# Block maxima in a table in one PSUM bank, with seven banks left for everything else

## Chip, cores and metric

The kernel runs on one core of one Trainium2 chip. The metric is the device time of one execution in microseconds (us); three runs of the kernel before took 3574.15, 3577.49 and 3579.05 us, so the median is 3577.49. The engines are TensorE (PE: matmuls; PEld: its weight loads), VectorE (DVE), ScalarE (ACT), GpSimd (POOL) and SyncE (SP, which issues most DMAs). TensorE writes its results to PSUM, which has eight banks of 512 fp32 columns by 128 partitions; VectorE and ScalarE read and write PSUM, GpSimd does not in this kernel.

## Reference

Four cross-attention layers in a row on a state `x` of 4 batches x 512 positions x 256 channels, all in fp32, all against one context of 1024 positions x 512 channels for each batch. Layers 0, 2 and 3 are alike: 16 heads of 64, with a bias on a few context positions.

```python
q = hidden_states @ Wq                       # 256 -> 16 * 64
k = encoder_hidden_states @ Wk               # 512 -> 16 * 64
v = encoder_hidden_states @ Wv
logits = jnp.einsum('bhqd,bhkd->bhqk', q, k) * scale
logits = logits + col_bias[None, None, :, :]
probs = jax.nn.softmax(logits, axis=-1)
out = jnp.einsum('bhqk,bhkd->bhqd', probs, v)
...
out = out @ Wo + bo + residual
```

Layer 1 normalises `x` by its root mean square first and has 16 query heads of 16 in 4 groups, each group with one key and value head ("grouped" attention). It has no bias on positions.

The softmax needs a number to subtract before the exponential. Any number that is the same for all 1024 context positions of one query and head will do, if it keeps the exponentials in range. This kernel takes a maximum.

## The kernel before

**Units.** A unit is two heads of a masked layer (0, 2, 3), or four heads of the grouped layer done as two runs of the same shape; a layer of a batch has eight units, so there are 96 masked and 32 grouped units (`units`, L44). A unit's logits are kept transposed: context positions on the partitions, in eight blocks of 128 (`NT`), and in a block 1024 columns, 512 queries for each of two heads. So one block of one unit is a tile of 128x1024, two PSUM banks.

**Steps.** The kernel is one long list of 96 steps, written out by hand (`order`, L70, and the loop at L1183). In step n the masked unit `g` is scored, the masked unit of the step before, `g1`, is attended, and weights and projections for later units fill TensorE's time. In 32 of the steps (12 to 19, 22 to 29, 32 to 39, 68 to 75) a grouped unit `lam` is attended too, and in most of these the logits of the next grouped unit, `coming`, are made. Each engine runs its instructions in the order in which the program issues them. The loop holds an estimated clock `now`: the items of `fill` run one after the other, subtractions and exponentials are issued as `events` when `now` passes their due time, logits pairs (`pairs`) are due from 12.0 on, 2.5 apart, and the work in `late` (scaling of attention outputs) is issued when the events are through, at the first logits pair or at the end of the step.

**One masked unit, in the order of a step:**
- `scores` (L832): for each of the eight blocks a matmul for each head into a pair of banks (L841), for block 0 also the bias (L847), a copy to SBUF by ScalarE (`g.st[t]`, L851). Block 0's pair is kept: VectorE takes the maximum of it and each later block in place (L855).
- `max_quarters` (L896) makes one maximum out of that pair for each 32 columns: L892 reduces 1024 columns to 32 with a 32x32 transposition, and seven small instructions (L902 to L909) combine the four quarters of the partitions. `max_everywhere` (L912) spreads the result over a pair of banks (L918), the "broadcast".
- `subtract` (L922): VectorE subtracts the broadcast from each block (L926); after the eighth the pair is given back. `exponentials` (L930): ScalarE (L932), and GpSimd adds the blocks up (L971).
- In the next step `attend` (L861): 16 matmuls into one bank, `g.po` (L871). Then, as `late` work, `normalise` (L1017): the sums are reduced in the same way as the maxima (`reciprocal_sums`, L892 and L1003 to L1011), spread (L1013), and the output is scaled (L1024), which gives `g.po` back.
- Two steps later `project_out` (L1027): two units together into a pair of banks (L1042), and VectorE adds the result to the state (L1060 or L1064).

**One grouped unit**: `logits_pair` (L813) makes two blocks at once, with two pairs of banks (L818), copies them (L824) and takes the maximum in place (L830); GpSimd subtracts (L924); `attend` puts it into one bank; `keep_even` (L881) and `keep_odd` (L883, L885) add the two halves of the output, and after every second unit `turn_grouped` (L973) divides by the sums, by transposing the output into a bank of its own and back (L982 to L988), and issues one or four DMAs on SP.

**Fill.** Projections of queries (`project_q`, L736), of keys (`k_part`, L525: four matmuls into one bank, in two items) and of values (`v_pair`, L571: likewise one bank for two items). In steps 41 to 64 and 77 to 92 keys and values of two units are made by seven products in place of eight from combined weights and contexts (`seven_products`, L624, L639); these hold two or three single banks at once.

**Banks.** All of PSUM is one tensor, `ps_all`. A `Place` (L101) takes one bank or an aligned pair, `back` gives it back. Both happen while the program is written, so the choice is fixed; on the chip the first writer of a bank waits until the last reader of its former use is done. The chooser takes what was given back longest ago:

```python
if width == 2:
    at = min(
        (n for n in range(0, 8, 2) if n in free and n + 1 in free),
        key=lambda n: max(free[n], free[n + 1]),
    )
else:
    at = min(free, key=lambda n: free[n] + (2 if n ^ 1 in free else 0))
```

`free` maps a bank to the count of returns at which it came back; a single bank whose neighbour is free too is put two returns later. Ties go to the bank that came back first.

Of the kernel before, what the change touches and what calls it, by code (L numbers as in the profile page):

```python
# [12 lines left out]
ALU = mybir.AluOpType  # L13
AX = mybir.AxisListType
PSUM = bass.MemoryType.PSUM

P = 128
B, S, C = 4, 512, 256
T, CT = 1024, 512
NI = S // P  # L20
NT = T // P
# [59 lines left out]
def kernel(ctx: ExitStack, tc: tile.TileContext, a: dict, out: bass.AP):  # L81
    nc = tc.nc
# [8 lines left out]
    def t_(shape, tag, name, bufs=1, dtype=FP):  # L91
        return sb.tile(shape, dtype, tag=tag, name=name, bufs=bufs)
# [2 lines left out]


    ps_all = ps.tile([P, 8, S], FP, tag="ps", name="ps")
    given_back = dict.fromkeys(range(8), 0)
    returns = [0]

    class Place:  # L101
# [26 lines left out]
    def take_set(g):  # L128
        g.set = sets_free.pop(sets_free.index(min(sets_free)))
        g.st = [st_slot((NT + 1) * g.set + t) for t in range(NT)]  # L130
        g.mx = st_slot((NT + 1) * g.set + NT)
# [681 lines left out]
    def logits_pair(g, i):  # L813
        ws = [Place(), Place()]
        for odd in range(2):
            for j in range(2):
                rows = slice(64 * odd + 32 * j, 64 * odd + 32 * (j + 1))
                nc.tensor.matmul(  # L818
                    ws[odd].ap[:, j * S : (j + 1) * S], lhsT=g.kt[rows, i * P : (i + 1) * P],
                    rhs=g.qt[rows, :], start=True, stop=True,  # L820
                )
        for odd, w in enumerate(ws):
            t = 2 * i + odd
            nc.scalar.copy(g.st[t], w.ap)  # L824
            if t == 0:
                g.mx_place = w
            else:
                w.back()
                top = g.mx_place.ap
                nc.vector.tensor_tensor(top, top, g.st[t], ALU.max)  # L830

    def scores(g):  # L832
        take_set(g)
        g.mx_place = Place()
        for t in range(NT):

            w = Place() if t else g.mx_place
            m = w.ap
            keys = slice(t * P, (t + 1) * P)
            for j in range(2):  # L840
                nc.tensor.matmul(  # L841
                    m[:, j * S : (j + 1) * S], lhsT=g.kt[g.rows[j], keys], rhs=g.qt[g.rows[j], :],
                    start=True, stop=t > 0,
                )
            if t == 0:
                for j in range(2):
                    nc.tensor.matmul(  # L847
                        m[:, j * S : (j + 1) * S], lhsT=aug_k[g.l][g.rows[j], keys],
                        rhs=aug_q[g.rows[j], :], start=False, stop=True,
                    )  # L850
            nc.scalar.copy(g.st[t], m)  # L851
            if t:
                w.back()
                top = g.mx_place.ap
                nc.vector.tensor_tensor(top, top, g.st[t], ALU.max)  # L855

    def place_out(g, width=1):
        g.place = Place(width)
# [24 lines left out]
    def keep_odd(g):  # L883
        half = gq[g.b, "o"][64 * g.h : 64 * (g.h + 1), :]
        nc.vector.tensor_tensor(half, half, g.po[64:128, :], ALU.add)  # L885
        g.place.back()

    def over_quarter(out_, of, op):
        nc.vector.tensor_reduce(  # L892
            out_, of.rearrange("p (b x) -> p b x", x=32), AX.X, op, apply_transpose=True
        )

    def max_quarters(g):  # L896
        w = Place(1)
        quarter, half = w.ap[:, 0:32], w.ap[0:64, 32:64]
        other = t_([64, 32], "other_max", f"other_max_{g.name}")
        over_quarter(quarter, g.mx_place.ap, ALU.max)  # L900
        g.mx_place.back()
        nc.vector.tensor_copy(other, quarter[64:128, :])  # L902
        nc.vector.tensor_tensor(half, quarter[0:64, :], other, ALU.max)
        nc.vector.tensor_copy(other[0:32, :], half[32:64, :])
        g.every = t_([P, 2 * S // 32, 1], "every", f"every_{g.name}")
        for h in range(4):
            nc.vector.tensor_tensor(  # L907
                g.every[32 * h : 32 * (h + 1), :, 0], half[0:32, :], other[0:32, :], ALU.max
            )  # L909
        w.back()  # L910

    def max_everywhere(g):  # L912
        if g.masked:
# [57 lines left out]
        nc.gpsimd.tensor_tensor(g.acc, g.st[0] if t == 1 else g.acc, g.st[t], ALU.add)  # L971

    def turn_grouped(g):  # L973
        w = Place(1)
        normalise_grouped(g, w.ap)
        w.back()

    def normalise_grouped(g, m):

        o = gq[g.b, "o"]  # L980
        short = t_([P, S // 32, 1], "short", f"short_{g.name}")
        nc.vector.transpose(m, o)  # L982
        nc.vector.reciprocal(short, m.rearrange("p (c r) -> p c r", r=32)[:, :, 16:17])
        nc.vector.transpose(
            m.rearrange("p (c r) -> p c r", r=32), short.to_broadcast([P, S // 32, 32])
        )
        g.ot = o
        nc.vector.tensor_tensor(o, o, m, ALU.mult)  # L988
        if g.u % 4 == 1:
            nc.sync.dma_start(out=o_kept, in_=o)  # L990
        else:
            for i in range(4):
                nc.sync.dma_start(
                    out=o[32 * i + 16 : 32 * (i + 1), :], in_=o_kept[32 * i : 32 * i + 16, :]
                )

    def reciprocal_sums(g, m):

        quarter, half = m[:, 0:32], m[0:64, 32:64]
        other = t_([64, 32], "other", f"other_{g.name}")  # L1000
        short = t_([P, S // 32, 1], "short", f"short_{g.name}")
        over_quarter(quarter, g.acc, ALU.add)
        nc.vector.tensor_copy(other, quarter[64:128, :])  # L1003
        nc.vector.tensor_tensor(half, quarter[0:64, :], other, ALU.add)
        nc.vector.tensor_copy(other[0:32, :], half[32:64, :])
        for h in range(4):
            cols = slice(h // 2 * S // 32, (h // 2 + 1) * S // 32)
            nc.vector.tensor_tensor(
                short[32 * h : 32 * (h + 1), :, 0], half[0:32, cols], other[0:32, cols], ALU.add
            )  # L1010
        nc.vector.reciprocal(short, short)  # L1011
        g.ot = t_([P, S], "ot", f"ot_{g.name}", bufs=3)
        nc.vector.transpose(  # L1013
            g.ot.rearrange("p (c r) -> p c r", r=32), short.to_broadcast([P, S // 32, 32])
        )

    def normalise(g):  # L1017
        w = Place(1)
        reciprocal_sums(g, w.ap)
        w.back()  # L1020
        scale_out(g)

    def scale_out(g):
        nc.vector.tensor_tensor(g.ot, g.po, g.ot, ALU.mult)  # L1024
        g.place.back()
# [76 lines left out]
    def at(n):  # L1102
        return steps[n] if 0 <= n < len(steps) else (None, None)
# [79 lines left out]
    for n in range(len(steps) + 2):  # L1183
        g, lam = at(n)
# [74 lines left out]
        def pair(i):  # L1259
            if i == 0:  # L1260
                behind_exponentials()
                take_set(coming)
            logits_pair(coming, i)
            if i == NT // 2 - 1:
                max_quarters(coming)
                max_everywhere(coming)
# [11 lines left out]
        if g:  # L1278
            g.now = NT if masked_at(g.n + 1) else 4
            scores(g)  # L1280
# [5 lines left out]
        if g:  # L1286
            max_quarters(g)
            max_everywhere(g)
        if g1 and g:
            attend(g1)  # L1290
            give_set(g1)
            if not ending:
                late.append(lambda: normalise(g1))
        elif g1:
            attend_last(g1)
            adds = [project_out(*each) for each in outs]
            outs = []
            reciprocal_rows(g1.ot, g1.psum, g1.mx)
            scale_out(g1)
            for add in adds:  # L1300
                add()
# [42 lines left out]
        if lam:  # L1344

            def attend_grouped():
                while any(of is lam for _, of, _ in events):
                    events.pop(0)[2]()
                lam.v = head(lam).v
                place_out(lam)  # L1350
                attend(lam)
                give_set(lam)
                late.append(lambda: keep_odd(lam))
                if lam.h == 1:
                    late.append(lambda: turn_grouped(lam))
# [81 lines left out]
```

## Time and profile before

| | us |
|---|---|
| median of three runs | 3577.49 |
| the profiled execution, as timed | 3576.7 |
| its span in the profile | 3574.9 |
| TensorE busy | 3470.4 |
| VectorE busy | 3036.3 |
| GpSimd busy | 2488.9 |
| ScalarE busy | 2331.6 |

The profiled execution lies within the runs. Lengths of steps, from one bias matmul (L847) to the next: 28.7 us for the plain even steps 42 to 64, 31.7 to 33.7 for the odd ones between, 40 to 42 for even steps with a grouped unit, 50 to 53 for odd ones.

The blocks of instructions of the change, from the groups by line (count, mean ns):

| line | what | count | mean |
|---|---|---|---|
| L855, L830 | maximum of two blocks, in place in PSUM | 672 + 224 | 1232, 1233 |
| L892 | reduction of 1024 columns from PSUM (maxima) | 128 | 1265 |
| L892 | the same from SBUF (sums) | 93 | 1253 |
| L902 to L904 | quarters of the maxima | 3 x 128 | 181 to 193 |
| L907 | last step of the quarters | 512 | 180 |
| L982, L984 | turning the grouped output | 16 each | 727 |

In the views below a line of a group reads: line, engine, operation, what it writes from what, shapes, count, busy us, mean ns, idle time of the engine ahead of it and who ended that. A line of the timeline reads: start us, length us, engine, line, operation, count of merged instructions, and in brackets the idle time ahead of the first. A line of the waits reads: who waited, for whom, us in total, times, longest.

### The profile page before, as it was taken

The page shows a single profiled execution, that of the slowest core. Times are in us where ns is not written, and L with a number is a line of the kernel's source. Part 1 is how long each engine was busy: PE and PEld are TensorE (multiplying, and loading weights), DVE is VectorE, ACT ScalarE, POOL GpSimd, SP SyncE. Part 2 cuts the span into 40 slices and gives each one's busy share as a digit, 9 for nine tenths or more (in the row PEclk, how much of TensorE's full clock was granted, in tenths as well). Part 3 has the DMA queues.
Part 4 walks back from the last instruction along what each step waited for, and adds up shares of the span by engine and source line. Part 5 has one row for each costly group of instructions (what it writes and reads, how often), then busy time and mean ns, then how long its engine had stood idle before and what let it go on. Part 6 is the DMA issues. An engine that isn't in the chain of part 4 may idle for free.

```text
span 3574.9 us, 42639 instructions
## 1 busy us (share of the span) xinstructions
PE 3470.4 (97%) x15262; PEld 1701.6 (48%) x15262; DVE 3036.3 (85%) x4166; ACT 2331.6 (65%) x2701; POOL 2488.9 (70%) x1241
## 2 busy tenths in 40 slices
PE   8999999999999999999999999999999999999998
PEld 4454544445444454444454545454544445454553
DVE  7778788887888878898888888888789888888887
ACT  4565577775777757777566666665677775666664
POOL 3565477774777747777678778767477776769774
PEclk9999999999999999999999999999999999999999
DMA  3222201002100030101001111010201011002110
GB/s 102 62 87 89 75 18 51 27 20 72 42 27 27 20 93 21 27 27 44 29 27 51 33 33 51 27 48 24 69 25 45 26 36 46 23 27 74 33 31 7
DMA packets 146201, 151.70 MB, mean 42 GB/s; under 512 B 23608, under 2 KB 123448, under 8 KB 145476
## 3 DMA queue, kind: packets, MB, share of 16 engines
q1 hardware_dynamic: 142894, 140.05, 12.6%
q0 software_dynamic: 2560, 8.39, 0.7%
q8 instruction: 121, 1.98, 0.2%
q14 instruction: 92, 0.75, 0.1%
q10 hardware_dynamic: 534, 0.52, 0.1%
HBM read 132.15 MB, written 15.73 MB: 41 GB/s over the span
## 4 chain that ended last, share of the span: by engine, by line
PE 78%; DVE 18%; ACT 2%; issue 2%; POOL 0%; DMA 0%; DVEq 0%; ACTq 0%; POOLq 0%
PE ps L871 16%; PE ps L841 15%; PE ps L639 13%; PE ps L584 10%; PE ps L536 10%; PE ps L818 5%; DVE st L926 5%; DVE ps L855 5%; PE ps L742 4%; PE ps L1042 3%; DVE ps L892 2%; DVE ps L830 1%; DVE every L907 1%; PE ps L719 1%; DVE ps L918 1%
## 5 line engine op out<-in xcount | busy, mean ns | idle before, releaser
L971 POOL TENSOR_TENSOR st<-st 128x1024 f32<-128x1024 f32 x668 | 1580.6, 2366 | 687.9 <-ACT st L932 643.0
L932 ACT ACTIVATE st<-st 128x1024 f32<-128x1024 f32 x1024 | 1037.0, 1056 | 320.7 <-DVE st L926 238.9
L855 DVE TENSOR_TENSOR ps<-ps,st 128x1024 f32<-128x1024 f32 x672 | 827.6, 1232 | 258.3 <-ACT st L851 197.4
L926 DVE TENSOR_TENSOR st<-st,ps 128x1024 f32<-128x1024 f32 x768 | 883.4, 1215 | 3.3
L924 POOL TENSOR_TENSOR st<-st 128x1024 f32<-128x1024 f32 x256 | 597.3, 2381 | 354.4 <-DVE st L918 306.1
L871 PE MATMUL ps<-st,v 128*64 128x512 f32 (+1 forms) x4064 | 790.9, 596 | 0.0
L851 ACT COPY st<-ps 128x1024 f32<-128x1024 f32 x768 | 717.1, 1046 | 104.3 <-PE ps L847 62.7
L841 PE MATMUL ps<-qt,kt 64*128 64x512 f32 x3072 | 723.5, 604 | 42.6 <-DVE ps L892 25.5
L841 PEld LDWEIGHTS ps<-qt,kt 64*128 64x128 f32 x3072 | 307.1, 187 | 401.2 <-issue 123.2
L871 PEld LDWEIGHTS ps<-st,v 128*64 128x64 f32 (+1 forms) x4064 | 240.8, 130 | 528.4 <-issue 428.3
L536 PE MATMUL ps<-ctx,wk 128*128 128x512 f32 x896 | 425.8, 624 | 2.2 <-ACT ctx L416 2.2
L584 PE MATMUL ps<-wv,ctx 128*128 128x256 f32 x1792 | 405.9, 382 | 0.0
L830 DVE TENSOR_TENSOR ps<-ps,st 128x1024 f32<-128x1024 f32 x224 | 276.1, 1233 | 144.3 <-ACT st L824 134.1
L584 PEld LDWEIGHTS ps<-wv,ctx 128*128 128x128 f32 x1792 | 336.8, 190 | 96.1 <-issue 53.3
L824 ACT COPY st<-ps 128x1024 f32<-128x1024 f32 x256 | 247.6, 1014 | 130.7 <-PE ps L818 129.0
L536 PEld LDWEIGHTS ps<-ctx,wk 128*128 128x128 f32 x896 | 171.9, 198 | 247.3 <-issue 231.0
L639 PE MATMUL ps<-st 128*128 128x128 f32 (+1 forms) x1200 | 229.0, 339 | 6.3 <-ACT ps L662 6.3
L818 PE MATMUL ps<-qt,kt 32*128 32x512 f32 x1024 | 196.4, 666 | 29.7 <-DVE ot L1024 24.9
L654 ACT COPY st<-ps 128x512 f32<-128x512 f32 x40 | 23.4, 585 | 301.6 <-PE ps L639 301.6
L639 PEld LDWEIGHTS ps<-st 128*128 128x128 f32 x1200 | 158.7, 192 | 74.7 <-issue 68.7
L742 PE MATMUL ps<-x,wq 128*128 128x512 f32 x384 | 186.6, 609 | 4.0 <-ACT st L824 2.3
L1042 PE MATMUL ps<-ot,wo 128*128 128x512 f32 x384 | 175.8, 600 | 0.7 <-DVE ot L1024 0.7
(178 smaller groups left out, 2740.5 us busy)
## 6 DMA issues: line engine op xcount, KB each, us to landing
ctx<-kept SPq DMA_DIRECT2D x24, 1024.0 KB
wk<-in_L_xattn_Wk_dram SPq DMA_DIRECT2D x47, 512.0 KB
wv<-in_L_xattn_Wv_dram SPq DMA_DIRECT2D x47, 512.0 KB
wq<-in_L_xattn_Wq_dram SPq DMA_DIRECT2D x96, 128.0 KB
wo<-in_L_xattn_Wo_dram SPq DMA_DIRECT2D x96, 128.0 KB
st<-kept SPq DMA_DIRECT2D x4, 2048.0 KB
qt<-q SPq DMA_DIRECT2D x64, 128.0 KB
kept<-st SPq DMA_DIRECT2D x12, 512.0 KB
```

The lines of the kernel that those rows point to most:

```text
L536: nc.tensor.matmul(m, lhsT=g.w["k"][:, k, :], rhs=ctx_half[g.b, n][:, k, :], start=(k == 0), stop=(k == KT - 1),)
L584: nc.tensor.matmul(m[:, half * 2 * P : (half + 1) * 2 * P], lhsT=ctx_half[g.b, t // 4][:, k, t % 4 * P : (t % 4 + 1) * P], rhs=g.w["v2"][: ...
L639: nc.tensor.matmul(m if is_keys else m[:, q], lhsT=right[:, k, :] if is_keys else left_[:, k, q], rhs=left_[:, k, :] if is_keys else right ...
L818: nc.tensor.matmul(ws[odd].ap[:, j * S : (j + 1) * S], lhsT=g.kt[rows, i * P : (i + 1) * P], rhs=g.qt[rows, :], start=True, stop=True,)
L841: nc.tensor.matmul(m[:, j * S : (j + 1) * S], lhsT=g.kt[g.rows[j], keys], rhs=g.qt[g.rows[j], :], start=True, stop=t > 0,)
L851: nc.scalar.copy(g.st[t], m)
L855: nc.vector.tensor_tensor(top, top, g.st[t], ALU.max)
L871: nc.tensor.matmul(g.po[at, :], lhsT=g.v[:, t, rows], rhs=g.st[t][:, j * S : (j + 1) * S], start=(t == first), stop=(t == last),)
L924: nc.gpsimd.tensor_tensor(g.st[t], g.st[t], g.mb, ALU.subtract)
L926: nc.vector.tensor_tensor(g.st[t], g.st[t], g.mb, ALU.subtract)
L932: nc.scalar.activation(st, st, AF.Exp)
L971: nc.gpsimd.tensor_tensor(g.acc, g.st[0] if t == 1 else g.acc, g.st[t], ALU.add)
```

## The change

One PSUM bank, number 7, is taken out of the chooser. Its first 256 columns are a table `tops` of 32 x 8, and four areas of 32 columns follow for the small trees. Each block's maxima are reduced at once, from the copy in SBUF, into column t of the table (`block_max`); the pair of banks of block 0 is given back like all others. `max_quarters` reduces the table (256 columns to 32) and takes no bank, `reciprocal_sums` takes none either. `turn_grouped` uses the bank of the grouped unit's own output, which `keep_odd` therefore gives back only for the first unit of two.

```diff
-    given_back = dict.fromkeys(range(8), 0)
+    given_back = dict.fromkeys(range(7), 0)
...
@@ logits_pair
             nc.scalar.copy(g.st[t], w.ap)
-            if t == 0:
-                g.mx_place = w
-            else:
-                w.back()
-                top = g.mx_place.ap
-                nc.vector.tensor_tensor(top, top, g.st[t], ALU.max)
+            w.back()
+            block_max(g, t)
...
     def scores(g):
         take_set(g)
-        g.mx_place = Place()
         for t in range(NT):
-
-            w = Place() if t else g.mx_place
+            w = Place()
...
             nc.scalar.copy(g.st[t], m)
-            if t:
-                w.back()
-                top = g.mx_place.ap
-                nc.vector.tensor_tensor(top, top, g.st[t], ALU.max)
+            w.back()
+            block_max(g, t)
...
     def keep_odd(g):
         half = gq[g.b, "o"][64 * g.h : 64 * (g.h + 1), :]
         nc.vector.tensor_tensor(half, half, g.po[64:128, :], ALU.add)
-        g.place.back()
+        if g.h == 0:
+            g.place.back()
...
+    tops = ps_all[:, 7, 0:256].rearrange("p (b t) -> p b t", t=NT)
+    most, most_half, added, added_half = (
+        ps_all[:, 7, 256 + 32 * n : 288 + 32 * n] for n in range(4)
+    )
...
+    def block_max(g, t):
+        over_quarter(tops[:, :, t], g.st[t], ALU.max)
+
     def max_quarters(g):
-        w = Place(1)
-        quarter, half = w.ap[:, 0:32], w.ap[0:64, 32:64]
+        g.every = t_([P, 2 * S // 32, 1], "every", f"every_{g.name}")
+        quarter, half = most, most_half[0:64, :]
         other = t_([64, 32], "other_max", f"other_max_{g.name}")
-        over_quarter(quarter, g.mx_place.ap, ALU.max)
-        g.mx_place.back()
+        nc.vector.tensor_reduce(quarter, tops, AX.X, ALU.max)
...
-        w.back()
...
     def turn_grouped(g):
-        w = Place(1)
-        normalise_grouped(g, w.ap)
-        w.back()
+        normalise_grouped(g, g.place.ap)
+        g.place.back()
...
-    def reciprocal_sums(g, m):
-        quarter, half = m[:, 0:32], m[0:64, 32:64]
+    def reciprocal_sums(g):
+        quarter, half = added, added_half[0:64, :]
...
     def normalise(g):
-        w = Place(1)
-        reciprocal_sums(g, w.ap)
-        w.back()
+        reciprocal_sums(g)
         scale_out(g)
```

`over_quarter` (L891) is unchanged: `nc.vector.tensor_reduce` of 1024 columns in groups of 32 with a transposition. `normalise_grouped` (L978) is unchanged too.

More of the change, by code (lines that the diff above doesn't have):

```diff
@@ L904, in max_quarters @@
         nc.vector.tensor_copy(other[0:32, :], half[32:64, :])
-        g.every = t_([P, 2 * S // 32, 1], "every", f"every_{g.name}")
         for h in range(4):
```

## The prediction

> **What bounds the kernel now.** I read the page's totals and chain first, then TensorE's waits, then step by step the granted clock, and last the timeline around the longest waits.
>
> ```profile
> span 3574.9 us, 42639 instructions
> PE 3470.4 (97%) x15262; PEld 1701.6 (48%) x15262; DVE 3036.3 (85%) x4166; ACT 2331.6 (65%) x2701; POOL 2488.9 (70%) x1241
> ...
> PE 78%; DVE 18%; ACT 2%; issue 2%; POOL 0%; DMA 0%; DVEq 0%; ACTq 0%; POOLq 0%
> ```
>
> TensorE sets the end, and VectorE is the one engine that interrupts it. TensorE's idle time is 104.5 us (3574.9 less 3470.4). Most of it has four causes, in the waits of TensorE (total, times, longest):
>
> ```profile
> PE ps L841 <- DVE ps L892: 25.5, 17, 1.8
> PE ps L818 <- DVE ot L1024: 24.9, 12, 2.8
> PE ps L841 <- ACT st L824: 11.4, 12, 1.0
> PE ps L818 <- DVE o L885: 4.8, 4, 1.4
> ```
>
> All four are waits for a PSUM bank. The first: the scores of a masked unit (L841) need the pair of banks in which the running maximum of the grouped unit still stands, until L892 has read it. The second: the logits of a grouped unit (L818) need the bank of the attention output, until L1024 has scaled it. I asked for the twelve odd steps in which a grouped unit is attended and another one's logits are made (13, 15, 17; 23, 25, 27; 33, 35, 37; 69, 71, 73), each from one bias matmul L847 to the next:
>
> ```profile
> 1476.90:1528.90 52.00, 47.12 (x178) 17.04 (x176) 44.63 (x61) 34.30 (x38) 35.16 (x15) 0.93 0.07 16
> ...
> sum 620.30, PE 572.27 PEld 209.31 DVE 534.59 ACT 413.40 POOL 421.99; mean PE 47.69 PEld 17.44 DVE 44.55 ACT 34.45 POOL 35.17
> ```
>
> The columns are length, busy time of the five engines, granted clock, DMA. TensorE is idle for 48.0 us in these twelve steps, and its clock is 0.93 in ten of them and 0.97 in two, where other steps have 1.00: 10 x 52 x 0.07 + 2 x 50 x 0.03 = 39 us lost. The timeline of one such step (start, length) shows both:
>
> ```profile
> 1475.90 1.13 PE L841 MATMUL ps<-qt,kt 64*128 64x512 f32 x4 [0.95 <-ACT st L824]
> ...
> 1479.87 1.13 PE L841 MATMUL ps<-qt,kt 64*128 64x512 f32 x4 [1.77 <-DVE ps L892]
> ...
> 1482.56 9.22 DVE L855 TENSOR_TENSOR ps<-ps,st 128x1024 f32<-128x1024 f32 x7
> ...
> 1510.86 2.79 PE L818 MATMUL ps<-qt,kt 32*128 32x512 f32 x4 [2.77 <-DVE ot L1024]
> ...
> 1513.58 3.47 PE L536 MATMUL ps<-ctx,wk 128*128 128x512 f32 x4
> ```
>
> After the wait of 2.77 us four matmuls take 3.47 us, which take 1.98 us elsewhere: the clock has dropped. The masked steps without a grouped unit (41 to 64, 77 to 92) have hardly any idle time and can't gain.
>
> **VectorE's tree, old and new.** Per group of eight blocks the old tree is seven L855 (or L830) and one L892; the new one is eight reductions of 128x1024 from SBUF and one of 256 elements.
>
> ```profile
> L926 DVE TENSOR_TENSOR st<-st,ps 128x1024 f32<-128x1024 f32 x768 | 883.4, 1215 | 3.3
> L855 DVE TENSOR_TENSOR ps<-ps,st 128x1024 f32<-128x1024 f32 x672 | 827.6, 1232 | 258.3 <-ACT st L851 197.4 <-DVE ps L855 0.9 <-ACT st L932 0.5
> ...
> L892 DVE TRANSPOSE_TENSOR_REDUCE ps<-ps 128x32 f32<-128x1024 f32 x128 | 161.9, 1265 | 12.1
> L892 DVE TRANSPOSE_TENSOR_REDUCE ps<-st 128x32 f32<-128x1024 f32 x93 | 116.5, 1253 | 3.9 <-ACT kt L541 3.9
> ...
> L226 DVE TENSOR_REDUCE first<-st 128x12 f32<-128x144 f32 x1 | 0.3, 303 | 0.0
> ```
>
> The block reduction costs 1253 ns (the sum's L892 reads SBUF likewise). The last reduction isn't in the trace: no less than L226's 303 ns (144 elements), no more than 1253 (1024). L226 is nearest; with the slope from L251 (12 elements, 165 ns) to it, 1.05 ns an element, 256 make 420 ns, an estimate. In durations: 8 x 1.253 + 0.42 = 10.44 us against 7 x 1.232 + 1.265 = 9.89, so 0.55 us more a group, 70 us over 128 groups, on an engine 85% busy.
>
> The distance between instructions decides more. Seven L855 back to back take 9.22 us: each starts (9.22 - 1.232) / 6 = 1.331 us after the last, 0.10 more than its duration, because it reads what that one wrote. Eight L926, independent, take 9.14 us in the step after: 1.132 apart, 0.08 less than their duration. A block reduction writes a column of its own and reads nothing of its predecessor. If it runs like L926 it comes every 1.17 us, if like L855 every 1.36. I take 1.17, since the dependency that stretches L855 is gone, and keep 1.36 for the range. Then a backlogged tree lasts 8 x 1.17 + 0.08 + 0.03 + 0.42 = 9.9 us instead of 10.6 (L855's start to L892's end): 0.7 earlier, and the grouped unit's tail ahead of it (1.25 + 0.42 behind the last copy, instead of 1.23 + 1.27) another 0.8. With 1.36 the tree is 0.7 us longer and the two cancel.
>
> The Trainium skill speaks against this edit (VectorE: DVE Perf Modes, "The DRAIN you can't avoid"): VectorE flushes its pipeline after each instruction whether a semaphore follows or not, so one should count instructions. Nine in place of eight would then lose 0.55 us a group; by that rule L885 would come no earlier, the even steps below would pay 34 us instead of 14 and the products 18 instead of none, and the sum would be 3560. The rows of L926 disagree: they overlap by 83 ns.
>
> **Banks.** I followed the chooser (lines 102-119) by hand with seven banks. The scores use three pairs in turn, as before, but no pair is held by a maximum. The attention output takes bank 6, the only one without a free neighbour. The broadcast maximum takes the pair of block 5, so until the last subtraction L926 the fill has two pairs where it had two pairs and a single.
> - Start of odd steps: the pair under L892 doesn't exist any more, and the first scores find the third pair free. The waits for L892 (25.5) and for L824 (11.4) go. L892's cover in the old code was none: TensorE stood.
> - Logits in odd steps: the first call gets the keys' pair, long copied out, and the broadcast's. The wait for L1024 goes, but the pair is free only after the last subtraction (0.3 us of waiting), and the second call takes the same two pairs again and waits for ScalarE's copies, which stand behind the exponentials: by the timeline some 1.5 us. 12 x 1.8 = 22 us come back. In steps 23 and 71, where the projection of queries goes to the end of the fill, that call meets the grouped output's bank, given back only after the turning (L988, 2.6 us behind L885): 2 x 4 = 8.
> - Logits in even steps: by a tie the grouped output lands in the queries' pair, and the second block waits for keep_odd (L885), which it didn't before:
>
> ```profile
> 1463.50 1.94 PE L818 MATMUL ps<-qt,kt 32*128 32x512 f32 x8
> ...
> 1466.12 0.69 DVE L885 TENSOR_TENSOR o<-o,ps 64x512 f32<-64x512 f32 x1
> ```
>
> L885 ends at 1466.81, and 1.6 us earlier with the shorter tree: 1465.2. The first block is through at 1464.0. 12 steps x 1.2 = 14 us. Behind the waiting L818 on TensorE stand the value products L584 and the other logits, and ScalarE's L824 and the block reductions wait for it in turn; with some 2 us of slack before the next step's tree they come late by no more than the wait itself.
> - Products with combined weights in the thirteen odd steps that don't load a new context: the second product now falls into the bank of the output projection and waits for its addition on VectorE:
>
> ```profile
> 1818.68 1.88 PE L639 MATMUL ps<-ctx,wk 128*128 128x512 f32 x4
> ...
> 1819.32 1.40 DVE L1060 SCALAR_TENSOR_TENSOR x<-ps,colL_xattn_bo,x 128x512 f32<-128x512 f32 x2
> ```
>
> The product starts at 1818.68. The first addition ends 0.70 us after 1819.32, 1.3 too late; in steps with L1064 it is 1.9. In these steps the tree starts with block 0's copy, 1 us earlier than now, and ends 1.7 us earlier: nothing to some 0.2 us remains. Without that gain (1.36) it costs 18 us.
> - The quarters' and the turning's own banks fall away: TensorE's waits for L907 (4.0 us) go. The turning keeps the grouped bank 2.6 us longer, counted above. No DMA moves, and SP's queue has the same issues behind L988.
>
> **Sum.** Against: 48.0 idle and 39 of clock in the odd steps, 11.4 at their starts (ahead of L847, so not in the 48), 7 for the four L892 waits in steps 19, 29, 39 and 75, 4.8 for L885: 110 us. Left or new: 22 + 8 + 14 = 44, and the clock. Waits of 1.4 us in the even steps drop no clock now, waits of 0.93 in the odd ones mostly do, so half of those steps pay 2 to 3 us again: 15. Gain 110 - 59 = 51, with 4 for L907: 55 us. The profiled execution took 3576.7 us (span 3574.9 and 1.8 around it), 0.8 below the median of 3577.49: **3522 us**. Its own range is 3485 (the new waits don't show) to 3555.
>
> **Rivals.**
> - VectorE waits for itself between block reductions, as at L855 (1.36 apart). For it: all eight write one bank, and the program may order accesses by bank; VectorE is 86% busy in the odd steps (534.59 of 620.30). Against: no read follows. The wait sits in every tree and decides from 1.3 us apart. L885 is then 1.6 us later: 12 x 2.8 = 34 in the even steps, the odd ones wait for the last subtraction 12 x 1.6 more = 19, 18 at the products, all the clock loss stays (39, and 15 more in the even steps), besides 44 - 14 = 30. 114 - 155 = -41: 3618, slower.
> - The waits move more than I count: the tree is quick, but ScalarE's copies, L885 and L988 hold TensorE half as long again (66 us for 44), and the clock pays 20 for 15. 114 - 86 = 28: 3549. For it: VectorE and ScalarE are both full around the first logits. Against: the copies alone need 1.93 us a pair, which the fill between two calls nearly covers.
> - Nothing measurable: VectorE, at 81 of 93 us over two steps, paces the grouped steps, and its 0.55 us a group cancel the banks: 3575.
>
> **How the numbers follow.** Forecast 0.50, moved waits 0.12, nothing 0.10, self-wait 0.28. Three runs spread over 0.14%, so 0.2% is what can be told from no change. Faster 0.62, same 0.10, slower 0.28. From 3482, below the forecast's own end, to 3610, which leaves out the worse half of the self-wait.
>
> **What would show it.** Right: no TensorE wait for L1024 and none for the reduction at the start of odd steps; block reductions under 1.2 us apart; clock of 0.97 or more in the odd steps; their length near 46 to 47 us instead of 52. Wrong: reductions 1.36 apart, waits of L818 for L885 or L988 over 2 us, waits of L639 for L1060 or L1064, or a step length of 28.7 us in the plain even steps that grows.

## The result, and the profile after

The change made the kernel slower: 3605.79 us (3604.84 to 3609.05, four executions) against 3576.06 us for the kernel before in the same series, a ratio of 1.0084 [1.0067, 1.0101]. The forecast was 3522 us and faster. What happened is the rival to which the prediction gave 0.28, VectorE waiting for itself between block reductions (3618). The range given, 3482 to 3610, holds the time, but only by that rival's part of it. The profiled execution took 3609.05 us, the slowest of the four. Two executions of later kernels, of 9098 and 9921 us, ran in a slow state and are left out everywhere.

In the changed kernel the block reduction is L890, the reduction of the table L901, keep_odd L877, the subtraction L924, the exponential L930, the additions after the output projection L1055 and L1059. The head and the chain of its page:

```profile
span 3607.3 us, 42805 instructions
PE 3482.6 (97%) x15262; PEld 1672.1 (46%) x15262; DVE 3113.3 (86%) x4294; ACT 2337.2 (65%) x2701; POOL 2489.2 (69%) x1241
...
PE 51%; DVE 40%; ACT 6%; issue 3%; DVEq 0%; POOL 0%; DMA 0%; ACTq 0%; POOLq 0%
DVE ps L890 18%; PE ps L639 11%; DVE st L924 10%; PE ps L835 9%; PE ps L863 8%; PE ps L584 8%; PE ps L536 6%; PE ps L742 3%; PE ps L818 3%; ACT st L845 3%; DVE ps L916 2%; ACT st L930 2%; DVE every L906 2%; PE ps L1037 1%; DVE ps L901 1%
```

VectorE holds 40% of the chain where it held 18%, and the block reduction alone is 18%. The waits of TensorE (who, for whom, us in total, times, longest):

```profile
PE ps L818 <- DVE o L877: 26.6, 12, 2.3
PE ps L536 <- DVE x L1059: 16.8, 10, 2.2
PE ps L863 <- ACT st L930: 16.0, 19, 1.5
PE ps L639 <- DVE x L1059: 12.2, 8, 1.8
PE ps L639 <- DVE x L1055: 5.4, 5, 1.4
PE ps L536 <- DVE x L1055: 5.4, 4, 1.7
```

The waits for the reduction at the start of the odd steps and for L1024 are gone, as forecast. In their place stand waits of the logits for keep_odd, of the keys and of the products with combined weights for the additions, and of the attention for exponentials. All are waits for something VectorE does behind a tree, the last by way of ScalarE, whose exponentials wait for VectorE's subtractions (L924). The group of the block reduction, one tree of eight, the exponentials behind it and the logits that wait for keep_odd after the subtractions, in the timeline (start, length; the idle time ahead in brackets):

```profile
L890 DVE TRANSPOSE_TENSOR_REDUCE ps<-st 128x32 f32<-128x1024 f32 x1117 | 1404.8, 1258 | 367.4 <-ACT st L845 172.6
```

```profile
1446.73 10.76 DVE L890 TRANSPOSE_TENSOR_REDUCE ps<-st 128x32 f32<-128x1024 f32 x8
...
1462.08 2.95 ACT L930 ACTIVATE st<-st 128x1024 f32<-128x1024 f32 x3 [2.37 <-DVE st L924]
...
1474.40 0.69 DVE L877 TENSOR_TENSOR o<-o,ps 64x512 f32<-64x512 f32 x1
```

```profile
1471.77 1.13 PE L818 MATMUL ps<-qt,kt 32*128 32x512 f32 x4
1475.14 1.71 PE L818 MATMUL ps<-qt,kt 32*128 32x512 f32 x4 [2.25 <-DVE o L877]
1476.78 3.78 PE L584 MATMUL ps<-wv,ctx 128*128 128x256 f32 x8
```

Eight reductions take 10.76 us, so they start (10.76 - 1.258) / 7 = 1.357 us apart, 0.10 more than one lasts. And the eight L584 after the wait take 3.78 us where they take 1.99 elsewhere: the clock has dropped, now in the even step. The same even and odd step as in the prediction, by the windows (length, busy time of the five engines, granted clock, then share and rate of the DMAs), before and after:

```profile
1435.88:1476.86 40.98, 40.03 (x200) 21.94 (x198) 36.36 (x51) 33.53 (x38) 35.20 (x15) 1.00 0.13 38
1476.86:1528.85 51.99, 47.11 (x176) 17.03 (x174) 44.62 (x61) 34.30 (x38) 35.16 (x15) 0.93 0.07 17
```

```profile
1441.91:1489.64 47.73, 44.12 (x200) 21.98 (x198) 38.77 (x54) 32.79 (x37) 35.14 (x15) 0.93 0.08 24
1489.64:1536.78 47.14, 44.80 (x176) 15.17 (x174) 44.33 (x61) 34.99 (x40) 35.17 (x15) 1.00 0.09 27
```

The odd step is 4.9 us shorter and has its full clock. The even step is 6.8 us longer and its clock is 0.93. All steps added up from the trace, each from one bias matmul to the next, with TensorE's idle time in brackets. The last row is what the clock cost: time multiplied by what the granted clock lacks of 1.00, as in the prediction. The last two columns belong to experiments below, the table in SBUF, and that with another penalty:

| steps | before | after | table in SBUF | and penalty |
|---|---|---|---|---|
| 12 odd grouped | 620.2 (48.0) | 560.1 (23.0) | 535.6 (5.3) | 535.7 (5.4) |
| 16 even grouped | 657.7 (16.5) | 728.6 (41.9) | 663.6 (13.8) | 635.2 (7.8) |
| 20 odd, masked only | 646.1 (6.9) | 664.8 (23.6) | 640.7 (3.2) | 644.4 (5.9) |
| 20 even, masked only | 574.5 | 574.5 | 574.5 | 574.5 |
| clock, odd and even grouped | 37.5 and 0 | 5.1 and 32.4 | 0 and 10.2 | 0 and 0 |

Asked for in narrow windows, the granted clock is either 1.00 or 0.50. In the even step above it is 0.50 from 1475.55 to 1482.38, which costs 3.4 us, and 1.00 in the rest of the step.

Idle time and clock are not all. Without idle time the 16 even steps take 641.2 us before, at a clock of 1.00, and 627.4 in the last column, at the same clock. Most of the difference is in the logits (L818): 82.9 us before, 71.8 in the last column. The prediction's row of the even step shows eight of them in 1.94 us, where other rows show 1.14. After the change they take 101.0 us, part of it clock. So some of the waiting stands in the trace as longer matmuls; what makes them longer was not tried.

The change took 60 us out of the odd steps, put 71 into the even ones and 19 into the odd masked-only steps. That is +30, and everything else adds 3, between the two profiled executions (3574.9 and 3607.3 us).

### The profile page after: what moved, and what is told of

The parts are those of the page before. It is cut to its first block, busy times and chain, and to the rows that moved or that the text cites. A ratio compares the mean times of both kernels' runs of the same rounds, so it can differ in the third digit from the quotient of the medians.

```text
span 3607.3 us, 42805 instructions
## 1 busy us (share of the span) xinstructions
PE 3482.6 (97%) x15262; PEld 1672.1 (46%) x15262; DVE 3113.3 (86%) x4294; ACT 2337.2 (65%) x2701; POOL 2489.2 (69%) x1241
## 4 chain that ended last, share of the span: by engine, by line
PE 51%; DVE 40%; ACT 6%; issue 3%; DVEq 0%; POOL 0%; DMA 0%; ACTq 0%; POOLq 0%
DVE ps L890 18%; PE ps L639 11%; DVE st L924 10%; PE ps L835 9%; PE ps L863 8%; PE ps L584 8%; PE ps L536 6%; PE ps L742 3%; PE ps L818 3%; ACT st L845 3%; DVE ps L916 2%; ACT st L930 2%; DVE every L906 2%; PE ps L1037 1%; DVE ps L901 1%
## 5 line engine op out<-in xcount | busy, mean ns | idle before, releaser
L890 DVE TRANSPOSE_TENSOR_REDUCE ps<-st 128x32 f32<-128x1024 f32 x1117 | 1404.8, 1258 | 367.4 <-ACT st L845 172.6
L930 ACT ACTIVATE st<-st 128x1024 f32<-128x1024 f32 x1024 | 1040.4, 1055 | 398.8 <-DVE st L924 257.2
L924 DVE TENSOR_TENSOR st<-st,ps 128x1024 f32<-128x1024 f32 x768 | 883.3, 1215 | 3.3
L863 PE MATMUL ps<-st,v 128*64 128x512 f32 (+1 forms) x4064 | 816.9, 598 | 17.6 <-ACT st L930 16.0
L835 PE MATMUL ps<-qt,kt 64*128 64x512 f32 x3072 | 707.2, 599 | 1.2 <-ACT qt L747 0.7
L863 PEld LDWEIGHTS ps<-st,v 128*64 128x64 f32 (+1 forms) x4064 | 243.9, 130 | 571.6 <-issue 492.5
L835 PEld LDWEIGHTS ps<-qt,kt 64*128 64x128 f32 x3072 | 279.3, 185 | 370.0 <-ACT st L845 183.4
L536 PE MATMUL ps<-ctx,wk 128*128 128x512 f32 x896 | 414.5, 607 | 24.5 <-DVE x L1059 16.8
L584 PE MATMUL ps<-wv,ctx 128*128 128x256 f32 x1792 | 422.6, 393 | 0.7 <-ACT qt L747 0.7
L584 PEld LDWEIGHTS ps<-wv,ctx 128*128 128x128 f32 x1792 | 346.5, 196 | 111.5 <-issue 64.3
L824 ACT COPY st<-ps 128x1024 f32<-128x1024 f32 x256 | 248.0, 1016 | 112.8 <-PE ps L818 110.4
L536 PEld LDWEIGHTS ps<-ctx,wk 128*128 128x128 f32 x896 | 165.4, 191 | 261.6 <-issue 202.1
L818 PE MATMUL ps<-qt,kt 32*128 32x512 f32 x1024 | 189.6, 676 | 31.3 <-DVE o L877 26.6
L747 ACT ACTIVATE qt<-ps 128x512 f32<-128x512 f32 x96 | 56.3, 587 | 114.8 <-PE ps L742 114.8
```

Of the source, the lines that this page charges most:

```text
L536: nc.tensor.matmul(m, lhsT=g.w["k"][:, k, :], rhs=ctx_half[g.b, n][:, k, :], start=(k == 0), stop=(k == KT - 1),)
L584: nc.tensor.matmul(m[:, half * 2 * P : (half + 1) * 2 * P], lhsT=ctx_half[g.b, t // 4][:, k, t % 4 * P : (t % 4 + 1) * P], rhs=g.w["v2"][: ...
L818: nc.tensor.matmul(ws[odd].ap[:, j * S : (j + 1) * S], lhsT=g.kt[rows, i * P : (i + 1) * P], rhs=g.qt[rows, :], start=True, stop=True,)
L835: nc.tensor.matmul(m[:, j * S : (j + 1) * S], lhsT=g.kt[g.rows[j], keys], rhs=g.qt[g.rows[j], :], start=True, stop=t > 0,)
L863: nc.tensor.matmul(g.po[at, :], lhsT=g.v[:, t, rows], rhs=g.st[t][:, j * S : (j + 1) * S], start=(t == first), stop=(t == last),)
L890: nc.vector.tensor_reduce(out_, of.rearrange("p (b x) -> p b x", x=32), AX.X, op, apply_transpose=True)
```

## The experiments

Eleven kernels were run, in three series. The time of the kernel before in them was 3579.26, 3577.88 and 3577.45 us.

**The table in SBUF.** The one edit that takes the own wait away if it has to do with the bank; everything else is the change.

```diff
-    tops = ps_all[:, 7, 0:256].rearrange("p (b t) -> p b t", t=NT)
+    def table(g):
+        return g.mx[:, 0:256].rearrange("p (b t) -> p b t", t=NT)
...
-        over_quarter(tops[:, :, t], g.st[t], ALU.max)
+        over_quarter(table(g)[:, :, t], g.st[t], ALU.max)
...
-        nc.vector.tensor_reduce(quarter, tops, AX.X, ALU.max)
+        nc.vector.tensor_reduce(quarter, table(g), AX.X, ALU.max)
```

> The table moves from bank 7 to 256 columns of the unit's own spare slot in SBUF (g.mx); bank 7 stays kept for the small trees, so the banks and their order are those of the changed kernel. Theory 1 (VectorE waits for its own last write to bank 7 before each block reduction): reductions 1.17 us apart instead of 1.36, a backlogged tree of 9.9 us instead of 11.3, the waits for L1055 and L1059 (40 us) nearly gone and those for L877 (26.6) halved, time 3520 to 3550. Theory 2 (seven banks are too few): the same waits at the same places within a fifth, 3595 to 3606. Theory 3 (a transposing reduction can't overlap the next): spacing stays at 1.26 or more, time 3570 to 3606.

Measured: 3478.94 us, 0.9717 [0.9701, 0.9733]: 127 us under the changed kernel, 100 under the kernel before in the same series, and 41 below the lower end of the first theory's range. The block reduction is L892 here; its group, its timeline and TensorE's waits:

```profile
L892 DVE TRANSPOSE_TENSOR_REDUCE st<-st 128x32 f32<-128x1024 f32 x1024 | 1175.7, 1212 | 324.3 <-ACT st L845 223.4
```

```profile
1390.07 9.09 DVE L892 TRANSPOSE_TENSOR_REDUCE st<-st 128x32 f32<-128x1024 f32 x8
```

```profile
PE ps L818 <- DVE o L877: 13.8, 12, 1.6
PE ps L818 <- ACT st L824: 4.4, 12, 0.5
```

(9.09 - 1.212) / 7 = 1.125 us apart. In the changed kernel each block reduction waits for ScalarE's semaphore and for VectorE's own, and the gap between two in a backlog is +104 ns (median). Here only ScalarE's is waited for, and the gap is -78. The waits for an addition are gone but for 0.6 us (L536) and 0.4 us, and the one for keep_odd is halved.

**Table and small trees in SBUF, eight banks.** The same, with the quarters and halves of maxima and sums in SBUF as well, and bank 7 given to the chooser.

```diff
-    given_back = dict.fromkeys(range(7), 0)
+    given_back = dict.fromkeys(range(8), 0)
...
-        quarter, half = most, most_half[0:64, :]
+        quarter, half = g.mx[:, 256:288], g.mx[0:64, 288:320]
...
-        quarter, half = added, added_half[0:64, :]
+        quarter, half = g.ot[:, 0:32], g.ot[0:64, 32:64]
```

> Table and small trees in SBUF, the chooser has all eight banks again. Theory 1: as the table in SBUF alone or up to 30 us better, 3500 to 3550. Theory 2: this one brings the gain, 30 us or more below the seven banks with the table in SBUF. If neither: within 0.2% of 3605.

Measured: 4214.22 us, 1.1774 [1.1755, 1.1794]. Not the banks, but the small instructions made it so. One group of it and GpSimd's main one, from its page, then the same small group (L1007) where its inputs lie in PSUM and SBUF, from the kernel with the other penalty:

```profile
L968 POOL TENSOR_TENSOR st<-st 128x1024 f32<-128x1024 f32 x668 | 1581.5, 2368 | 1107.8 <-ACT st L929 1064.3
L1005 DVE TENSOR_TENSOR short<-ot,other 32x16 f32<-32x16 f32 x372 | 445.5, 1198 | 6.9
```

```profile
L1007 DVE TENSOR_TENSOR short<-ps,other 32x16 f32<-32x16 f32 x372 | 61.1, 164 | 6.9
```

In the trace, the copy of the maxima (L901) lasts 177 ns in the 89 cases in which GpSimd is idle and 2138 ns in the 39 in which it runs. The reductions with one input (L900) take 420 ns either way. The section "Who interferes with whom" of the Trainium skill's page "SBUF — State Buffer" says that VectorE and GpSimd share a pair of SBUF ports, which a copy can lock for the whole instruction and through which an operation with two SBUF inputs reads its second one. These rows agree: 2138 ns is nearly one instruction of GpSimd (2368), and L900, with its one input, is not slowed. The kernel says nothing on the number of banks.

**Table in SBUF, small trees in borrowed banks, eight banks.** The first experiment with bank 7 given back; quarters and halves in a `Place(1)`, as in the kernel before.

```diff
-    given_back = dict.fromkeys(range(7), 0)
+    given_back = dict.fromkeys(range(8), 0)
...
-        quarter, half = most, most_half[0:64, :]
+        w = Place(1)
+        quarter, half = w.ap[:, 0:32], w.ap[0:64, 32:64]
```

> The table in SBUF, eight banks, the small trees in banks that they take and give back as in the kernel before; grouped outputs turned in their own bank. Theory 1: 1.17 us apart, within 15 us of the kernel with the trees in SBUF, 3500 to 3560. Theory 2: the small trees' own banks cost TensorE waits again (L906 some 4 us), otherwise the same.

Measured: 3483.1 us, 0.973 [0.9714, 0.9747], 4 us from the first experiment with overlapping intervals, and again below the ranges expected. So the kept bank is worth nothing measurable in sum: it costs the chooser a bank and saves it the borrowing. The sum hides a trade. With eight banks the 16 even grouped steps take 624.2 us without idle time (663.6 with seven), and the 12 odd ones 576.9 (535.6). Of the 27.2 us of idle time in those odd steps 18.9 are in this wait:

```profile
PE ps L835 <- DVE every L906: 28.4, 12, 2.4
```

The scores wait for the bank of the quarters; 4 us had been expected.

**The turning alone**, put into the kernel before.

```diff
-        g.place.back()
+        if g.h == 0:
+            g.place.back()
...
-        w = Place(1)
-        normalise_grouped(g, w.ap)
-        w.back()
+        normalise_grouped(g, g.place.ap)
+        g.place.back()
```

> The kernel before with one part of the change: the grouped output is turned in its own bank, which is given back after the turning. Both theories: within 0.2% of before, 3570 to 3584; if the longer hold costs as I reckoned for steps 23 and 71, up to 10 us more.

Measured: 3550.96 us, 0.9919 [0.9902, 0.9935], 28 us under the kernel before in the same series and outside both expectations. Of the 24.9 us of waits of L818 for L1024, 1.4 are left. Two kinds of smaller waits took their place, 16.4 us, none longer than 1.0; the one for L885 was there before (4.8 us):

```profile
PE ps L818 <- DVE o L988: 10.2, 10, 1.0
PE ps L818 <- DVE short L1008: 6.2, 7, 1.0
PE ps L818 <- DVE o L885: 5.2, 4, 1.4
```

The total of idle time fell from 104.5 us to 96.5, that of busy time by 16 (3470.4 to 3454.1). Some 10 of these 16 are clock: the granted mean went from 0.989 to 0.992.

**The changed kernel without the turning part** (the reverse of that diff).

> The changed kernel without its turning part: the accumulator goes back after each head again and the turning takes a bank of its own. Turning alone, put into the kernel before, took 28 us off. If its worth is in what it takes away and stands by itself, this kernel is 3625 to 3640 us, against 3605.8. If that gain came from the order in which banks come free there, which the seven banks and the table's place change anyway, it is 3598 to 3612 us.

Measured: 3663.5 us, 1.0232 [1.0215, 1.0249]. Neither reading held: the turning is worth 58 us here, more than in the kernel before. The bank of the turning, borrowed late, becomes the one for which the logits wait:

```profile
PE ps L818 <- DVE o L985: 56.7, 12, 6.0
PE ps L818 <- DVE o L877: 25.2, 12, 2.2
```

**Columns apart.** The table stays in bank 7, each block writes 32 columns side by side instead of every eighth.

```diff
-    tops = ps_all[:, 7, 0:256].rearrange("p (b t) -> p b t", t=NT)
+    tops = ps_all[:, 7, 0:256].rearrange("p (t b) -> p t b", t=NT)
```

> The table stays in bank 7, but block reduction t writes 32 columns beside each other (128 bytes per partition) where the change writes every eighth column; the small reduction reads the same 256 numbers across. No two block reductions then share even a range of addresses. The table in SBUF showed neighbouring reductions overlapping by 78 ns, the changed kernel shows them 104 ns apart. Theory A, VectorE waits for its own last write because it goes to the same bank: still about 1.36 us apart, 3605 us (3595 to 3615). Theory B, it waits because the written ranges interleave: no wait on its own semaphore is left among the eight, about 1.17 us apart, 3480 us (3465 to 3495). The small reduction, which took 432 ns, may change with the stride of its reading; 128 of them at 50 ns more or less would be 6 us.

Measured: 3603.51 us, 1.0071 [1.0055, 1.0088]; the gap is +104 ns, both semaphores are waited for, as in the changed kernel. Theory B falls: ranges that don't overlap wait all the same.

**Six rows of eight by themselves**, into columns of their own (n from 0 to 7 in each), ahead of the work of a kernel that has the table in SBUF and the other penalty, which is shown further below.

```diff
+    nc.vector.tensor_reduce(**probe_max(ps_all[:, 7, 32 * n : 32 * n + 32]))
...
+    nc.vector.tensor_reduce(**probe_max(ps_all[:, 6 + n % 2, 256 + 32 * n : 288 + 32 * n]))
...
+    nc.vector.tensor_reduce(**probe_max(st_all[:, 0, 1, 32 * n : 32 * n + 32]))
```

> The kernel with the table in SBUF and the other penalty (3456.6 us), with six rows of eight VectorE instructions put ahead of its work, when nothing else uses VectorE or PSUM: eight block reductions into one bank, eight into two banks by turns, eight into SBUF, then eight maxima of 128x64 into one bank, into two banks by turns and into SBUF; no two write the same columns. If the wait is a matter of the bank, the reductions into one bank start some 100 ns after the end of the one before, and those into two banks by turns and into SBUF some 80 ns before it. If it is a matter of writing PSUM at all, those into two banks by turns show the same 100 ns. If it belongs to reductions that turn blocks, the maxima show no difference between one bank and two; if it is a matter of every write, the maxima into one bank are further apart than those into two. The 48 instructions are some 45 us more: 3495 to 3505 us, less what the loads of the beginning hide.

Measured (start, length of eight): one bank, two banks by turns, SBUF, first for the block reduction, then for a maximum of 128x64.

```profile
2.11 10.32 DVE L151 TRANSPOSE_TENSOR_REDUCE ps<-st 128x32 f32<-128x1024 f32 x8
12.34 9.10 DVE L153 TRANSPOSE_TENSOR_REDUCE ps<-st 128x32 f32<-128x1024 f32 x8
21.35 9.09 DVE L155 TRANSPOSE_TENSOR_REDUCE st<-st 128x32 f32<-128x1024 f32 x8
30.37 2.06 DVE L157 TENSOR_TENSOR ps<-st 128x64 f32<-128x64 f32 x8
32.34 1.17 DVE L159 TENSOR_TENSOR ps<-st 128x64 f32<-128x64 f32 x8
33.43 1.16 DVE L161 TENSOR_TENSOR st<-st 128x64 f32<-128x64 f32 x8
```

It is the bank, for both kinds of write tried. Into one bank each instruction starts 35 ns after the end of the one before; into two by turns 91 ns (reductions) and 89 ns (maxima) ahead of it, about as into SBUF. The instructions into two banks carry a wait on VectorE's semaphore too from the second or third on, but they start before the one just ahead of them ends, so what they wait for lies further back and is done. The wait is the instruction's own, for a semaphore; whether the chip would need it was not tried. The expected size was wrong: 35 ns, not 100. In the kernel each block reduction waits for ScalarE's semaphore as well, and there the gap is 104; what the second semaphore does to it was not tried by itself. The whole took 3488.99 us in its one execution, 32 more than without, where 45 less what the loads hide had been expected.

**The table in SBUF for one kind of unit alone.** The grouped ones first, then the masked ones.

```diff
+    def table(g):
+        if g.masked:
+            return tops
+        return g.mx[:, 0:256].rearrange("p (b t) -> p b t", t=NT)
```

> The table in SBUF for the grouped units alone, in bank 7 for the masked ones. 32 of the 128 trees are grouped. If each tree's eight spacings cost the same wherever they stand (127 us over 128 trees, 1 us each), the time is 3605.8 - 32 = 3574 us. If the cost sits where VectorE is late in the twelve grouped pairs of steps, and both kinds of tree run there, more than that comes back: 3530 to 3560 us. If the masked trees alone set it, 3595 to 3606 us.

Measured: 3574.49 us, 0.9992 [0.9983, 1.0002], 31 us less than the changed kernel for 32 of the 128 trees.

> The table in SBUF for the masked units alone (96 of the 128 trees), in bank 7 for the grouped ones: the other half of the experiment with the grouped trees, which gave 31 us. If the cost of a tree stands by itself, this gives 127 - 31 = 96 us and the time is 3510 us (3503 to 3517). If the two kinds stand in each other's way, so that one tree's wait falls into the other's, it is 3480 to 3500 us.

Measured: 3517.5 to 3525.2 us, 0.9847 [0.9827, 0.9867]; the profiled execution took 3517.5, 88 us less than the changed kernel, for 96 trees; that is just above the first range expected. 31 + 88 = 119 of the 127 us that both give together, so the cost is close to 1 us for each tree of either kind. A tree's own loss is at most 8 x 0.182 = 1.46 us by the gaps, and two thirds of that reach the end.

**Another penalty in the chooser, with the table in SBUF.**

```diff
-                at = min(free, key=lambda n: free[n] + (2 if n ^ 1 in free else 0))
+                at = min(free, key=lambda n: free[n] + (2.5 if n ^ 1 in free else 0))
```

> The table in SBUF as in the first experiment (3478.9 us), and one more edit: the penalty of 2 that the bank chooser adds to a bank whose neighbour is free too becomes 2.5, so that a tie which went to one of two free banks goes to the bank that stands alone. In the first experiment 12 waits of L818 for the keep_odd copy (L877) were 13.8 us of TensorE's idle time, and they come from such a tie in the even grouped steps. If those waits are a matter of which bank is given: they go, and with the clock that they cost the time is 3455 to 3472 us. If VectorE is late as a whole there, another wait on VectorE takes their place, and the time is 3475 to 3485 us.

Measured: 3456.62 us (3456.12 to 3456.95), 0.966 [0.9644, 0.9676], the fastest kernel of this study, 3.4% under the kernel before. The waits of L818 for L877 are gone. Short waits of the attention for values took their place, beside which the clock stayed full:

```profile
PE ps L863 <- ACT v L591: 7.8, 12, 0.9
```

TensorE is busy for 99% of the span at a granted clock of 1.000.

**The same penalty with the table in bank 7**, the changed kernel otherwise.

> The changed kernel with the chooser's penalty of 2.5 alone, the table still in bank 7. With the table in SBUF this edit took 22 us off. If the waits of L818 for L877 (26.6 us here) are a matter of which bank is given, they go here too, and the time is 3570 to 3590 us. If VectorE is late there as a whole, another wait takes their place: 3598 to 3608 us.

Measured: 3579.0 us, 1.0006 [0.9996, 1.0016]. The time is in the first range, but its reason isn't: the waits for L877 went and another took their place.

```profile
PE ps L863 <- ACT v L591: 37.4, 12, 4.1
PE ps L536 <- DVE x L1059: 16.7, 10, 2.2
```

The attention waits for values whose copies (L591) stand on ScalarE behind exponentials, and these wait for VectorE's subtractions behind the long tree:

```profile
1440.88 2.95 ACT L930 ACTIVATE st<-st 128x1024 f32<-128x1024 f32 x3 [2.36 <-DVE st L924]
...
1444.20 3.90 ACT L930 ACTIVATE st<-st 128x1024 f32<-128x1024 f32 x4
1448.00 0.57 ACT L591 COPY v<-ps 128x512 f32<-128x512 f32 x1
```

```profile
1448.62 4.91 PE L863 MATMUL ps<-st,v 128*32 128x512 f32 x28 [3.95 <-ACT v L591]
```

The idle time of the 16 even steps is 43.0 us, against 41.9 in the changed kernel. Their length fell from 728.6 to 693.1 us all the same, so what was saved there is busy time: 36.7 us, of which 17 are clock (15.4 us lost against 32.4). The same even step as above, at 0.96 where it had 0.93:

```profile
1420.72:1465.11 44.39, 40.44 (x201) 20.61 (x198) 38.84 (x54) 32.84 (x37) 35.16 (x15) 0.96 0.08 25
```

The clock was 0.50 for 3.41 us here and for 6.83 us there. Why one wait of 4 us costs less clock than two of 1.4 and 2.3 us was not tried.

## Why the prediction was wrong, and where it was right

**The step that failed** is the spacing in the part on VectorE's tree: "I take 1.17, since the dependency that stretches L855 is gone". The distance is 1.357 us. The prediction put the gaps between the seven L855 down to reading what was just written, but a write to the same bank is enough, read or not. In the probe eight independent maxima into one bank start 35 ns after each other's end, and into two banks 89 ns before it. The reasoning compared the block reduction with L926, which is also independent, but L926 writes SBUF. The argument for the rival, that the program may order accesses by bank, stood in the text, and it was given 0.28 because "no read follows".

**The mechanism behind it was right, under the rival's number.** The prediction said that the self-wait decides from 1.3 us apart and named the places: the logits of the even steps, the products, the clock. All three came. The products were priced at 18 us, for thirteen steps; they wait 17.6 us in 13 waits. What the rival also named did not come: in the odd grouped steps it had 19 us of logits waiting for the last subtraction and 30 us from the forecast, and all the idle time there is 23.0 us. The wait for L885 (now L877) was priced at 12 x 2.8 = 34, and is 26.6 in 12 waits. The clock of the odd steps was expected to stay low; it rose nearly to full (37.5 us lost before, 5.1 after), and the even steps lost 32.4 us instead of none, where 15 had been priced. Not named were the keys' waits for the additions (L536, 22.2 us) and the attention's for the exponentials (L863, 16.0). The rival's 3618 is 12 us too high; that it is so near is in part luck, since terms that did not come stand against terms that it lacked.

**The forecast's sum, tried where its premise holds.** With the table in SBUF the reductions are 1.125 us apart, and the time is 3479, 43 us under the forecast of 3522:
- The waits for the reduction and for L1024, and the lost clock of the odd steps: gone as said; 48.0 us of idle time became 5.3.
- Logits in even steps, by a tie: 14 us forecast, 13.8 measured in 12 waits. That the tie causes them is shown, since the other penalty removes them.
- Logits in odd steps, 22 us, and steps 23 and 71, 8 us: mis-sized. The waits of L818 for L824 are 4.4 us in 12, where 1.5 us each had been read from the timeline, and none for the turning is left. Eight logits behind such a wait take 2.04 us in place of 1.14, so some of the rest stands as busy time. By the lengths of the steps the sum left 620.3 - 48.0 - 39 + 30 = 563 us for the twelve, ahead of any clock; they take 535.6. That is 28 of the 43 us.
- The clock, 15 us, for the odd steps: it costs nothing there and 10.2 us in the even ones, which the prediction had left at full clock.
- The masked-only steps, which "can't gain": the odd ones are 5.4 us shorter (646.1 to 640.7).
- Seven banks instead of eight, with the small trees in the kept one: no measurable difference in sum, but some 40 us moved between odd and even steps.

**The turning** was counted as small, with 8 us against it in steps 23 and 71. Alone it gains 28 us against the kernel before (3550.96 of 3579.26), and taking it out of the change costs 58. The prediction gave the end of the waits for L1024 to the new order of the banks as a whole; the turning alone already takes them from 24.9 to 1.4 us.

**The other rivals.** "Nothing measurable" is excluded by the interval. "The waits move more than I count" described the right kind of loss for the wrong reason: its 66 us of waits assume a quick tree.

## What to carry to other kernels

Before a series of independent instructions is given one PSUM bank to write, look whether any row of the profile shows two writes by one engine into one bank back to back; distinct columns don't make them independent. SBUF removed that wait here, and two banks by turns did in the probe, but a small copy or operation with two inputs that moves from PSUM to SBUF may then stand behind GpSimd. When a wait is taken from one step of a pipeline, price the next consumer of the same late engine at both spacings, since here the same idle time (65 us in odd and even grouped steps together, before and after) only changed its place.

## What the runs showed of the hardware

- A block reduction that waits for the semaphore of the one just before, as each one does in this program when both write one PSUM bank, starts 126 ns later than one into another bank (+35 against -91 ns in the probe), and lasts 1260 ns instead of 1217. The section "The DRAIN you can't avoid" of the Trainium skill's "VectorE: DVE Perf Modes" reports that eight copies with a semaphore after each took no longer than eight with one after the last. Here, eight reductions with a wait for the one just before took 10.32 us and eight without such a wait 9.10, and for these the measurement decides.
- A copy of 64x32 elements within SBUF takes 177 ns beside an idle GpSimd and 2138 ns beside a busy one, on average.
- Short waits of TensorE can cost nearly as much again in clock: in the 16 even steps the changed kernel had 41.9 us of idle time and lost 32.4 us more to a granted clock of 0.50, for 3.41 or 6.83 us at a time. In the step shown the waits ahead of it were of 1.36 and 2.25 us.
